# Reordering one step of a linear-attention stage: the next pair's maximum ahead of the last pair's sum, normed rows and keys ahead of the logits' copy, and a first load in two parts

## The chip, the cores and the metric

The kernel runs on one core of one Trainium2 chip. The metric is device time in microseconds (us) of one execution; lower is better. The core has a matrix engine (PE, with its weight loads shown apart as PEld), a vector engine (DVE), an activation engine (ACT), a general engine (POOL) and SP, which here only starts transfers. Each engine works through its own queue of instructions, and they wait for each other by semaphores.

## What is computed

The reference is a block of three residual layers over 4 x 2048 rows of 256 numbers: half of a mixture-of-experts layer, an attention layer, and half of the same mixture-of-experts layer again. The mixture layer sends every row to two of eight experts with a capacity; it is not touched here. The attention is of the linear kind: no row is compared with another row. Cut to what matters:

```python
q = _split_heads(x @ Wq + bq)            # 16 heads of 16 columns
v = _split_heads(x @ Wv + bv)
q = softmax(q, axis=-1) * s              # over the 16 columns of a head
k = softmax(q, axis=-2) * s              # over all rows of the batch
ctx  = einsum('bhnd,bhne->bhde', k, v)   # 16 x 16 per head and batch
attn = einsum('bhnd,bhde->bhne', q, ctx)
x = x + (attn @ Wo + bo)                 # x inside is the normed row
```

So `k` comes from `q`, and nothing of a batch can be given out before all 2048 of its rows have gone into `ctx`.

## The kernel before

The stages follow each other: the first router and the first expert stage (to about 921 us of the span), the attention (925 to 1171), the second routing, and the second expert stage. Only the attention is touched by the change.

There the 8192 rows lie as 64 tiles of 128 rows in `xw` (each 256 columns of the row and 16 of the second router's logits and weights). They are loaded from `acc`, the sum written by the first expert stage, in 16 transfers of four tiles each (L1124). The work goes in 32 pairs of tiles, eight pairs to a batch, by a loop over steps `i` that is a software pipeline: step `i` begins pair `i`, and holds later parts of the pairs before. The loop stands in a block of manual schedule for PE, DVE, ACT and POOL: what is emitted first comes first in the queue of its engine. The order of the calls in the loop is therefore the order of execution on each engine.

The parts, with their engines:

- `stats(2i+2, 2)`: mean and variance of the next pair's two tiles on DVE (L783, L784), then the inverse deviation on POOL (`ve` L157, `rstd` L158).
- `turn_x(i)`: four transposes of the rows on PE (`trx`, L791), copied by ACT (`xT`, L793).
- `project(i-1)`: eight matrix products on PE (`qp`, L799). `qp` has a single PSUM buffer of two banks; each bank holds 256 columns of q and 8 router logits of one tile.
- `logits_in(i-1)`: ACT copies the 8 logits a tile from `qp` into `xw` (L805).
- `largest(i-1)`: DVE scales and biases `qp` into `q` (two instructions, L810), takes the maximum of each head (`m`, L815), and POOL subtracts it (L816).
- `exp(i-2)`: ACT, in place (L819).
- `share(i-2)`: DVE sums the exponentials (`z`, L823) and inverts (`rz`, L825); POOL multiplies (L826). `q` is then the softmax.
- `keys(i-3)`: ACT takes the exponential of the softmax (`ek`, L832) and writes the two normed tiles into a ring of four (`xs`, L837).
- `turn_q(i-3)`: four transposes on PE (`trq`, L844), copied by ACT (`qT`, L846).
- `sums(i-3)`: eight products of keys and normed rows on PE, summed in `pc` over the eight pairs of a batch (L856).
- `context_1` to `context_4`: once per batch, from `pc` to the matrix `mo` (L867 to L906).
- `add_y(y)` and `take_y(y)` with `y = i - 12`: eight products on PE (`py`, L914, one buffer), added to `xw` by DVE (L924), with the statistics of the result (L926) and, every second pair, the norms on POOL.
- `choose_on`: the second router's choice, two of its small DVE steps at a time, and the norm of finished rows on ACT (L185).

So steps 3 to 11 carry everything but `add_y` and `take_y`; steps 12 to 31 carry all; the rest runs out.

Of the kernel before, what the change touches and what calls it, by code (L numbers as in the profile page):

```python
# [26 lines left out]
def macaron_kernel(  # L27
# [22 lines left out]
    nc = tc.nc  # L50
    B, N, D = x_in.shape
    E, _, F = wg.shape
    NJ = N // P
    T = B * NJ
# [15 lines left out]
    def tiles_of(ap):  # L70
        return ap.rearrange("(t p) d -> p t d", p=P)

    x_rows, out_rows = x_in.rearrange("b n d -> (b n) d"), out.rearrange("b n d -> (b n) d")
    x_tiles, out_tiles, acc_tiles = tiles_of(x_rows), tiles_of(out_rows), tiles_of(acc)
    JL = NJ // 4
# [15 lines left out]
        out=before, in_=ones, compare_op=ALU.is_gt, fill=0.0, base=0, pattern=[[1, P]], channel_multiplier=-1  # L91
# [4 lines left out]
        out=heads, in_=ones, compare_op=ALU.is_ge, fill=0.0, base=0,  # L96
# [3 lines left out]
        out=heads, in_=heads, compare_op=ALU.is_ge, fill=0.0, base=15,  # L100
# [36 lines left out]
    rstd = const.tile([P, T], F32, name="rstd")  # L137
# [13 lines left out]
    def spread(ap, shape):  # L151
        return ap.to_broadcast(shape)

    def deviation(var, n, pool, dst, scale=1.0):

        ve = pool.tile([P, NJ], F32, tag="ve", name="ve", bufs=4)
        nc.gpsimd.tensor_scalar(ve[:, :n], var, scale, EPS, ALU.mult, ALU.add)  # L157
        nc.gpsimd.tensor_tensor(dst, ve[:, :n], spread(minus_half, [P, n]), ALU.pow)  # L158
# [105 lines left out]
    def write_rows(xw, to, ts):  # L264
        nc.sync.dma_start(out=tiles_of(to)[:, ts, :], in_=xw[:, ts, :])
# [500 lines left out]
    def attention(xw, w, to, weights, pool, ppool):  # L766
# [7 lines left out]
        ring = []  # L774
# [5 lines left out]
        def stats(t, n):  # L780
            for i in range(t, t + n):
                st = pool.tile([P, 6], F32, tag="st", name="st", bufs=4)
                nc.vector.bn_stats(st, xw[:, i, 0:D])  # L783
                nc.vector.bn_aggr(mv[:, i, :], st)  # L784
            deviation(mv[:, t : t + n, 1], n, pool, rstd[:, t : t + n])
# [18 lines left out]
        def logits_in(i):  # L804
            nc.scalar.copy(xw[:, 2 * i : 2 * i + 2, D:W1], qp[i][:, :, D:W1])  # L805

        def largest(i):
            q = pool.tile([P, 2, D], F32, tag="q", name="q", bufs=5)
            for k in range(2):
                nc.vector.scalar_tensor_tensor(  # L810
                    q[:, k, :], qp[i][:, k, 0:D], rstd[:, 2 * i + k : 2 * i + k + 1], bqs, ALU.mult, ALU.add
                )
            qs[i] = q.rearrange("p k (h d) -> p (k h) d", d=H)
            m = pool.tile([P, 2 * H], F32, tag="m", name="m", bufs=3)
            nc.vector.tensor_reduce(m, qs[i], AX.X, ALU.max)  # L815
            nc.gpsimd.tensor_tensor(qs[i], qs[i], spread(m.unsqueeze(2), [P, 2 * H, H]), ALU.subtract)  # L816

        def exp(i):
            nc.scalar.activation(qs[i], qs[i], AF.Exp)  # L819

        def share(i):
            z = pool.tile([P, 2 * H], F32, tag="z", name="z", bufs=3)
            nc.vector.tensor_reduce(z, qs[i], AX.X, ALU.add)  # L823
            rz = pool.tile([P, 2 * H], F32, tag="rz", name="rz", bufs=3)
            nc.vector.reciprocal(rz, z)  # L825
            nc.gpsimd.tensor_tensor(qs[i], qs[i], spread(rz.unsqueeze(2), [P, 2 * H, H]), ALU.mult)  # L826

        def keys(i):


            eks[i] = pool.tile([P, 2, D], F32, tag="ek", name="ek", bufs=3)
            nc.scalar.activation(  # L832
                eks[i].rearrange("p k (h d) -> p (k h) d", d=H), qs[i], AF.Exp, scale=QSCALE
            )
            for k in range(2):
                t = 2 * i + k
                nc.scalar.mul(ring[i % 4][:, k, 0:D], xw[:, t, 0:D], rstd[:, t : t + 1])  # L837

        def turn_q(i):
            ps = ppool.tile([P, DC, 2, P], F32, tag="tr", name="trq", bufs=2)  # L840
# [24 lines left out]
        def context_1(b):  # L865
            rc = pool.tile([P, DC], F32, tag="rc", name="rc", bufs=2)
            nc.vector.reciprocal(rc, pcs[b][:, :, D])  # L867
            g = pool.tile([P, DC, D], F32, tag="g", name="g", bufs=1)
            nc.scalar.mul(g[:, 0, :], pcs[b][:, 0, 0:D], rc[:, 0:1])
            nc.vector.tensor_scalar(g[:, 1, :], pcs[b][:, 1, 0:D], rc[:, 1:2], None, ALU.mult)  # L870
            parts[b] = g
# [27 lines left out]
        def context_4(b):  # L899
            cxT = parts.pop(b)  # L900
            tag = "qp" if b == B - 1 else "py"
            ps = ppool.tile([P, 2, 2 * D], F32, tag=tag, name="mops", bufs=1)
            for k in range(DC):
                nc.tensor.matmul(ps[:, k, 0:W1], cxT[:, k, :], wox[:, k, :], start=True, stop=True)
            mo[b] = pool.tile([P, DC, W1], F32, tag="mo", name="mo", bufs=2)
            nc.vector.tensor_tensor(mo[b], ps[:, :, 0:W1], spread(box.unsqueeze(1), [P, DC, W1]), ALU.add)  # L906
# [34 lines left out]
        def choose_on(n, m, which=0):  # L941

            while len(choosing) > which and n:
                ts, steps, tiles = choosing[which]
                while n:
                    n -= 1
                    if next(steps, 0) == 0:
                        steps = None
                        break
                if steps is None and ts.stop > T - NJ:  # L950
                    chosen.append(choosing.pop(which))
                    continue
                for t in tiles[: m if steps else None]:
                    norm_row(xw, t)
                del tiles[:m]
                if steps is None:
                    write_rows(xw, to, ts)
                    choosing.pop(which)

        def has(i, n=NP):  # L960
            return 0 <= i < n

        LAST = NP + PB + 4
        with tc.manual_schedule(engines=ENGINES):
            stats(0, 2)
            for i in range(LAST):
                y = i - PB - 4

                b3 = (i - 3) // PB - 1 if (i - 3) % PB == 0 else -1
                b4 = (i - 4) // PB - 1 if (i - 4) % PB == 0 else -1  # L970
                if has(b3, B):
                    context_1(b3)
                if b3 == B - 1:
                    choose_on(1, 0)
                if has(b4, B - 1):
                    context_4(b4)
                if has(i - 2):
                    exp(i - 2)
                if has(i):
                    turn_x(i)  # L980
                if has(i - 2):
                    share(i - 2)
                if has(i + 1):
                    stats(2 * i + 2, 2)
                if has(i - 1):
                    project(i - 1)
                    logits_in(i - 1)
                if has(i - 3):
                    keys(i - 3)
                if has(b3, B):  # L990
                    context_2(b3)
                if b3 == B - 1:
                    choose_on(1, 0)
                if has(i - 1):
                    largest(i - 1)
                if has(i - 3):
                    turn_q(i - 3)
                ps = add_y(y) if has(y) else None
                if b3 == B - 1:
                    choose_on(3, 0)  # L1000
                if has(b3, B):
                    context_3(b3)
                if b3 == B - 1:
                    choose_on(2, 0)
                    context_4(b3)
                if has(i - 3):
                    sums(i - 3)
                if i < LAST - PB - 2:
                    choose_on(2, 2)
                if has(y):  # L1010
                    take_y(y, ps)
                if i >= LAST - PB:

                    choose_on({LAST - 3: 0, LAST - 2: 5, LAST - 1: 3}.get(i, 4), 0)
            while choosing:
                for k in reversed(range(len(choosing))):
                    choose_on(1, 0, k)
            for ts, _, tiles in chosen:
                for t in tiles:
                    norm_row(xw, t)  # L1020
                write_rows(xw, to, ts)
# [58 lines left out]
    with tc.tile_pool(name="w1", bufs=2) as wpool:  # L1080
        weights = {}
        with tc.tile_pool(name="r1", bufs=1) as pool, tc.tile_pool(name="r1p", bufs=2, space=PSUM) as ppool:
            xw = pool.tile([P, T, W], F32, name="xw")
# [36 lines left out]
    xw = kept.tile([P, T, W], F32, name="xw")  # L1120
    w = kept.tile([P, E, T], F32, name="w")
    with tc.tile_pool(name="at", bufs=1) as pool, tc.tile_pool(name="atp", bufs=1, space=PSUM) as ppool:
        for t in range(0, T, JL):
            nc.sync.dma_start(out=xw[:, t : t + JL, 0:D], in_=acc_tiles[:, t : t + JL, :])  # L1124
        attention(xw, w, rows[1], att_weights, pool, ppool)


# [41 lines left out]
```

## Time and profile before

| what | value |
|---|---|
| runs shown, median of 3 | 2053.22 us (2050.62 to 2053.68) |
| the profiled execution's own time | 2051.27 us |
| its span | 2049.4 us |
| PE, DVE, ACT, POOL busy over the span | 1879.1, 1413.5, 656.8, 882.3 us |
| mean granted clock of PE | 0.954 |
| loads of `xw` from `acc`, first issue | 924.97 us |
| first transposes of the attention | 928.95 us |
| first context product (L890) | 990.38 us |
| last product of `add_y` ends about | 1160.4 us |
| routing's first transposes (L282) | 1171.17 us |

The page of a profile sums over all stages, so busy shares of the whole span tell little of the 246 us in question. Times in the timeline are counted from the span's start. A line of the timeline has start, duration, engine, line, operation, tile written and tiles read, shapes, and in square brackets how long the engine had been idle and who ended that. Ends of matrix products are modelled.

### The profile page before, as it was taken

The numbers are of one execution on the slowest core, as the hardware profiler recorded it, in microseconds if no ns is written. First come the engines' busy times: TensorE is split into PE (matmuls) and PEld (weight loads), VectorE is DVE, ScalarE is ACT, GpSimd is POOL, SyncE is SP. The second block draws the span as 40 slices with busy tenths as digits, with TensorE's granted clock in tenths as the row PEclk, the third lists the DMA queues.
The fourth block names the chain that finished last, engine by engine and source line by source line (L and its number), as shares of the span: only waits on it lengthen the run. The fifth ranks groups of instructions, "written<-read, shape, count | busy, mean of one in ns | idle before, by whom it ended". The sixth has DMA issues, their size and how long they took to land.

```text
span 2049.4 us, 24693 instructions
## 1 busy us (share of the span) xinstructions
PE 1879.1 (92%) x9162; PEld 1439.7 (70%) x9162; DVE 1413.5 (69%) x2499; ACT 656.8 (32%) x1357; POOL 882.3 (43%) x737
## 2 busy tenths in 40 slices
PE   6379999999999999997999627999999999999998
PEld 4247777777777777775888415777777777777776
DVE  7867676767676766545789886767676666767654
ACT  5322322232223222224556503222322222232221
POOL 5335353535353535334556303535353535353533
PEclk8579999999999999998999858999999999999999
DMA  9912222223131322115012531223132323131211
GB/s 348 299 28 38 78 38 78 51 65 77 39 79 38 80 40 39 17 16 167 21 42 86 182 134 28 69 47 79 37 79 40 81 37 84 34 84 34 41 15 13
DMA packets 99910, 147.61 MB, mean 72 GB/s; under 512 B 7496, under 2 KB 86352, under 8 KB 99664
## 3 DMA queue, kind: packets, MB, share of 16 engines
q1 hardware_dynamic: 69056, 102.77, 14.8%
q0 software_dynamic: 30720, 43.27, 13.0%
q8 instruction: 72, 1.18, 0.2%
q14 instruction: 46, 0.38, 0.1%
q10 hardware_dynamic: 16, 0.01, 0.0%
HBM read 98.84 MB, written 55.57 MB: 75 GB/s over the span
## 4 chain that ended last, share of the span: by engine, by line
PE 83%; DVE 6%; POOL 2%; issue 1%; ACT 1%; DMA 1%; POOLq 0%; DVEq 0%; ACTq 0%; SPq 0%
PE mm L529 41%; PE mm L675 27%; PE one L529 7%; PE tr L476 2%; PE pc L856 2%; PE qp L799 2%; PE ix L399 1%; PE py L914 1%; DVE above L298 1%; DVE q L810 1%; DVE st L926 0%; DVE xw L924 0%; DVE cand L305 0%; DVE m L815 0%; PE trx L791 0%
## 5 line engine op out<-in xcount | busy, mean ns | idle before, releaser
L675 PE MATMUL mm<-wdt,h 128*128 128x256 f32 x2560 | 579.0, 381 | 0.0
L675 PEld LDWEIGHTS mm<-wdt,h 128*128 128x128 f32 x2560 | 475.9, 190 | 63.9
L561 POOL TENSOR_TENSOR h<-ct 128x1280 f32<-128x1280 f32 x96 | 279.0, 2906 | 424.7 <-ACT ct L558 421.5
L529 PE MATMUL mm<-xs,ws 128*128 128x320 f32 x1536 | 459.1, 435 | 2.2 <-DVE xs L482 2.0
L482 DVE TENSOR_TENSOR ct<-ct,mm 128x640 f32<-128x640 f32 x384 | 313.0, 818 | 104.2 <-PE mm L529 95.5
L529 PEld LDWEIGHTS mm<-xs,ws 128*128 128x128 f32 x1536 | 292.0, 191 | 127.0 <-issue 5.5
L558 ACT ACTIVATE ct<-ct 128x320 f32<-128x320 f32 (+1 forms) x224 | 181.8, 813 | 284.5 <-DVE ct L482 284.5
L482 DVE TENSOR_TENSOR ct<-p,mm 128x640 f32<-128x640 f32 x128 | 105.0, 821 | 238.5 <-ACT p L546 200.4
L482 DVE TENSOR_TENSOR ct<-u,mm 128x640 f32<-128x640 f32 x256 | 210.1, 821 | 59.7 <-PE mm L529 55.8
L546 ACT COPY p<-one 128x320 f32<-128x320 f32 x256 | 108.5, 424 | 406.4 <-PE one L529 404.2
L685 POOL DMA_INDIRECT out_dram<-eo,ixs x80 | 133.1, 1664 | 220.7 <-ACT eo L684 213.7
L685 POOL DMA_INDIRECT acc<-eo,ixs x80 | 132.8, 1661 | 221.1 <-ACT eo L684 214.1
L451 POOL DMA_INDIRECT r<-rows,ixs x160 | 158.6, 991 | 145.3 <-DVE ws L482 97.2
L684 ACT ACTIVATE eo<-mm,r 128x256 f32<-128x256 f32 x160 | 75.7, 473 | 396.5 <-PE mm L675 396.5
L529 PE MATMUL mm<-xsT,ws 128*128 128x320 f32 x512 | 158.7, 432 | 0.0
L390 DVE TENSOR_TENSOR lo<-count,slot_lo 128x1024 f16<-128x1024 int16 x112 | 128.3, 1220 | 0.0
L529 PEld LDWEIGHTS mm<-xsT,ws 128*128 128x128 f32 x512 | 97.3, 190 | 40.5
L482 DVE TENSOR_TENSOR u<-p,mm 128x640 f32<-128x640 f32 x128 | 104.9, 820 | 15.6 <-PE mm L529 12.5
L529 PE MATMUL one<-xsT,wgt 128*128 128x320 f32 x256 | 91.3, 439 | 0.0
L529 PE MATMUL mm<-xsT,wgt 128*128 128x320 f32 x256 | 91.1, 438 | 0.1
L529 PE MATMUL mm<-xsT,wut 128*128 128x320 f32 x256 | 90.9, 437 | 0.0
L529 PE MATMUL one<-xsT,wut 128*128 128x320 f32 x256 | 90.5, 435 | 0.0
(207 smaller groups left out, 2314.9 us busy)
## 6 DMA issues: line engine op xcount, KB each, us to landing
wgt<-in_L_ffn_wg_dram SPq DMA_DIRECT2D x16, 1024.0 KB, 5.0
wut<-in_L_ffn_wu_dram SPq DMA_DIRECT2D x16, 1024.0 KB, 7.0
wdt<-in_L_ffn_wd_dram SPq DMA_DIRECT2D x16, 1024.0 KB, 5.5
rows<-xw SPq DMA_DIRECT2D x7, 2176.0 KB, 10.6
xw<-in_L_attn_x_dram SPq DMA_DIRECT2D x16, 512.0 KB, 8.9
xw<-acc SPq DMA_DIRECT2D x16, 512.0 KB, 8.8
out_dram<-xw SPq DMA_DIRECT2D x16, 512.0 KB, 2.9
r<-rows,ixs POOLq DMA_INDIRECT x160
```

Source lines behind the costliest of these rows:

```text
L390: nc.vector.tensor_tensor(lo, spread(count.unsqueeze(1), shape), spread(at.unsqueeze(2), shape), ALU.is_equal)
L451: nc.gpsimd.indirect_dma_start(out=r, out_offset=None, in_=src[:, :], in_offset=bass.IndirectOffsetOnAxis(ap=lists[e][:, i : i + 1], axis=0),)
L476: nc.tensor.transpose(ps[:, (i - i0) * P : (i - i0 + 1) * P], got[k][i][:, c * P : (c + 1) * P], ident)
L482: nc.vector.tensor_tensor(o, a, b, op)
L529: nc.tensor.matmul(ps, a, b, start=True, stop=True)
L546: nc.scalar.copy(p1[p][:, m, :], one[:, :BH])
L558: nc.scalar.activation(ct[:, qs, 0, :], ct[:, qs, 0, :], AF.Silu)
L561: engine.tensor_tensor(hq[:, qs, :], ct[:, qs, 0, :], ct[:, qs, 1, :], ALU.mult)
L675: nc.tensor.matmul(po[i], hs[p][:, j, i * P : (i + 1) * P], weights[e][2][:, j * NF + p, :], start=(p == 0 and j == 0), stop=(p == NF - 1 ...
L684: nc.scalar.mul(eo, po[i], got[k][i][:, D + e : D + e + 1])
L685: ins = nc.gpsimd.indirect_dma_start(out=dst[:, :], out_offset=bass.IndirectOffsetOnAxis(ap=lists[e][:, i0 + i : i0 + i + 1], axis=0), in_ ...
L799: nc.tensor.matmul(qp[i][:, k, 0:W1], xT[i][:, k, c, :], wqx[:, c, :], start=(c == 0), stop=(c == DC - 1))
```

## The change

Three edits, all in the attention stage.

1. `share(i-2)` moves from before `stats` to behind `largest(i-1)`. On DVE the order of a step turns from z, rz, statistics, q, q, m to statistics, q, q, m, z, rz. On POOL the multiplication by `rz` moves from the head of the step to behind the subtraction of the maximum.
2. `keys(i-3)` moves from behind `logits_in(i-1)` to before `project(i-1)`, and inside it the two normed tiles are written before the exponential. On ACT the order of a step turns from exp, xT, logits' copy, ek, xs, xs, qT to exp, xT, xs, xs, ek, logits' copy, qT.
3. The first load of four tiles becomes two loads of two tiles each; there are 17 transfers instead of 16.

No instruction of an engine is added or taken away, PE's order stays, and nothing is computed otherwise.

```diff
         def keys(i):
+            for k in range(2):
+                t = 2 * i + k
+                nc.scalar.mul(ring[i % 4][:, k, 0:D], xw[:, t, 0:D], rstd[:, t : t + 1])
             eks[i] = pool.tile([P, 2, D], F32, tag="ek", name="ek", bufs=3)
             nc.scalar.activation(
                 eks[i].rearrange("p k (h d) -> p (k h) d", d=H), qs[i], AF.Exp, scale=QSCALE
             )
-            for k in range(2):
-                t = 2 * i + k
-                nc.scalar.mul(ring[i % 4][:, k, 0:D], xw[:, t, 0:D], rstd[:, t : t + 1])
...
                 if has(i):
                     turn_x(i)
-                if has(i - 2):
-                    share(i - 2)
                 if has(i + 1):
                     stats(2 * i + 2, 2)
+                if has(i - 3):
+                    keys(i - 3)
                 if has(i - 1):
                     project(i - 1)
                     logits_in(i - 1)
-                if has(i - 3):
-                    keys(i - 3)
...
                 if has(i - 1):
                     largest(i - 1)
+                if has(i - 2):
+
+                    share(i - 2)
                 if has(i - 3):
                     turn_q(i - 3)
...
-        for t in range(0, T, JL):
-            nc.sync.dma_start(out=xw[:, t : t + JL, 0:D], in_=acc_tiles[:, t : t + JL, :])
+
+        for t, n in [(0, 2), (2, 2)] + [(t, JL) for t in range(JL, T, JL)]:
+            nc.sync.dma_start(out=xw[:, t : t + n, 0:D], in_=acc_tiles[:, t : t + n, :])
```

## The prediction

> **What bounds the kernel now.** I read the views from the whole to the step. The page first: TensorE is busy 92% of the span and the chain that ended last is 83% PE, nearly all of it in the two expert stages that the change leaves alone. The attention stage runs from 924.97 us (first load) to about 1171, so whatever is won must come from 246 of 2049 us. Next, the busy times in stretches of 20 us (columns: stretch, length, then PE, PEld, DVE, ACT, POOL busy with counts, granted clock, DMA share, GB/s):
>
> ```profile
> 960.00:980.00 20.00, 17.01 (x88) 13.99 (x87) 13.32 (x36) 11.80 (x28) 10.57 (x15) 1.00 0.00 1
> ...
> 1020.00:1040.00 20.00, 20.00 (x107) 17.28 (x106) 16.66 (x44) 10.17 (x24) 12.08 (x22) 1.00 0.10 33
> ```
>
> There are two halves. From 1000 to about 1123 PE never rests (one step each 6.17 us: qp starts at 1000.62 and 1006.79). Only before, in the steps without add_y, and in the run-out does it have holes. The waits of PE name them:
>
> ```profile
> PE pc L856 <- ACT xs L837: 5.9, 8, 0.8
> ...
> PE qp L799 <- DVE q L810: 3.7, 2, 3.0
> ```
>
> Then the timeline of one early step, between two exponentials:
>
> ```profile
> 954.09 0.63 ACT L819 ACTIVATE q<-q 128x512 f32<-128x512 f32 x1 [1.63 <-POOL q L816]
> 954.62 0.57 ACT L793 COPY xT<-trx 128x512 f32<-128x512 f32 x1
> 954.75 0.69 DVE L823 TENSOR_REDUCE z<-q 128x32 f32<-128x512 f32 x1 [1.83 <-ACT q L819]
> ...
> 955.90 0.17 ACT L805 COPY xw<-qp 128x16 f32<-128x16 f32 x1 [0.71 <-PE qp L799]
> ...
> 955.97 0.63 ACT L832 ACTIVATE ek<-q 128x512 f32<-128x512 f32 x1
> ...
> 956.50 0.90 ACT L837 ACTIVATE xs<-xw,rstd 128x256 f32<-128x256 f32 x2
> ...
> 956.77 0.86 DVE L810 SCALAR_TENSOR_TENSOR q<-qp,rstd,bqs 128x256 f32<-128x256 f32 x2
> ...
> 957.05 2.00 PE L856 MATMUL pc<-xs,ek 128*128 128x257 f32 x8 [0.75 <-ACT xs L837]
> ...
> 957.66 0.69 DVE L815 TENSOR_REDUCE m<-q 128x32 f32<-128x512 f32 x1
> ...
> 958.43 1.06 POOL L816 TENSOR_TENSOR q<-q,m 128x512 f32<-128x512 f32 x1 [0.35 <-DVE m L815]
> ```
>
> Two loops of nearly one length turn here. On DVE: exp, z, rz, statistics (1.03), q, q, m, the subtraction on POOL, exp again: 954.09 to 959.52, 5.43 us. On PE: qp (1.95, its end to the copy .03), copy of the logits (its successor .07 later), ek (.53), first xs (.50 and .05), pc to trx 1.84, trx to qp .44: 5.41 us. PE alone needs 1.84 + .44 + 1.78 + .44 = 4.50 us by the same starts.
>
> One more look decides the forecast: what q waits for when DVE is free.
>
> ```profile
> 1014.95 0.17 ACT L805 COPY xw<-qp 128x16 f32<-128x16 f32 x1 [1.14 <-PE qp L799]
> ...
> 1015.22 0.88 DVE L810 SCALAR_TENSOR_TENSOR q<-qp,rstd,bqs 128x256 f32<-128x256 f32 x2 [0.23 <-POOL q L826]
> ```
>
> DVE had been idle since 1014.99 and qp ended at 1014.91, yet q starts .27 after the start of ACT's copy, .10 after its end. The same .27 stands at 935.02, 1002.87, 1009.04, 1021.39 and 1033.74, and no q starts before the copy of its step has ended. A DVE read of a PE result otherwise starts .04 after PE's end (py ends 1004.78, its sum starts 1004.82). The releaser named (POOL) had nothing for q: q waits for the logits' copy.
>
> **What the Trainium skill says.** "PSUM — Partial Sum Buffer", section "PSUM bank collisions raise a hardware error": two engines may not touch one bank together, a ScalarE read with a VectorE read included, so accesses must be held apart by semaphores. That fits: columns 0 to 255 (q) and 256 to 263 (copy) share qp's banks, and the trace shows the .27. "TensorE: Matmul & The Clock Gate", section "Architectural detail": ACT and DVE are strict FIFO; every row above agrees, so emission order is execution order. The same page, Part 1: after an idle window of about 3.4 us PE's clock halves. Here PE idles from 938.5 to 941.48 and the granted clock is 0.50 from 942 to 945; qp there takes 3.57 against 1.95. "DMA: Bandwidth & Descriptors", section "Anatomy of one DMA", gives about 2.0 us fixed for one transfer; here first issue to first use is 3.9 us, of which 0.52 MB at 350 GB/s is 1.5, leaving 2.4.
>
> **The change, part by part.**
>
> *Largest ahead of share.* Nothing is added. On DVE z and rz (.69 and .35) go behind q, q, m; on POOL the multiplication by rz goes behind the subtraction. q no longer waits for z, hence not for the exponential of the step before: the 5.43 loop on DVE is cut. What is later: q's final value by about 1.1 us after the subtraction (rz ends 2.65 after q's start, the product runs from 2.83 to 3.90). trq needs it in the next step, some 4 us after q at the earliest; ek needs it at 4.58 (below). Both are covered.
>
> *Keys ahead of the logits' copy.* On ACT the order becomes exp, xT, xs, xs, ek, copy, qT. pc no longer waits for qp's end by way of ACT, so the 5.41 loop is cut too. But the copy now stands behind exp, and q behind the copy. That closes a new loop, one step long: q to m .89, m .69, to the subtraction .08 to .14, the subtraction 1.06, to exp .03 (in all 2.77 at 935.02 to 937.79, 2.82 at 984.54 to 987.36); exp to xT .53, xT to the next .47, xs .40 and .40, ek .53 (2.33); copy to q .27. Sum 5.37 to 5.42. So both old loops are replaced by one just as long, and PE keeps about .7 us of hole in each early step. The steady pace gains only what DVE had slipped: q went from 945.90 to 984.54 in seven steps, 5.52 each; 7 x (5.52 - 5.39) = .9 us.
>
> *First rows in two transfers.* The first pair's data is half, .26 MB at 350 GB/s: .75 us earlier; bounds 0 (if both halves land together) and 1.0. One more issue costs SP .37 us while its queue is only these loads; the next tiles are needed a step later.
>
> *The start.* With the first rows .75 earlier, q of pair 0 starts at 934.27 and its exp at 937.04. Then xT 937.57, copy of pair 1 938.03 (qp of pair 1, behind q as before, ends about 937.32), q of pair 1 938.30 against 940.47 before, since z, rz and the statistics no longer stand ahead. Its exp 941.07, copy of pair 2 943.40, q 943.67 against 945.90: 2.23 us ahead, the .75 included. qp of pair 2 can start at 939.2, so the long idle and its half clock go too, but ACT's chain, not PE, ends last there; I count nothing for the clock.
>
> *Later steps.* 2.23 + .9 = 3.1 us ahead when the first context product starts (990.38 before). From there PE is the bound at 6.17, and the new loop of 5.4 fits under it with .75 to spare. In the steps with choosing, DVE is busy up to 93%; its order is only rotated, so the sum of y comes at the same place when DVE is behind. Twice the choosing's own exponential on ACT waits for DVE steps that now stand 1.04 later, which I bound at .5 us of PE each; I take 0, since PE's work ahead of pc (trq and py, 2.2 us) covers it. The other way, the waits of z for exp (.18 to .50 at six late steps) vanish, which helps only where DVE ends last; I take .3. In the run-out (1125 to 1134), where DVE is the bound, q must now wait for a copy, about .4 us lost. Sum: 3.1 - .4 + .3 = 3.0 us gained. What follows the attention shifts as a whole.
>
> Against the profiled execution (2051.27, span 2049.4) that is 2048.3. The median shown is 2053.22, 1.95 above it, so I say 2050.0.
>
> **Rivals.**
>
> *A, the bound moves as above*: -3.0, with 1.5 to 4.8 by the unknowns (transfer 0 to 1.0, clock phase ±1, choosing -1).
>
> *B, q isn't tied to the copy.* Then the loop is two steps long: q to exp 2.80, exp to pc 2.48, pc to the end of the next qp 4.23, 9.51 for two, 4.76 a step. pc of pair 0 would start at 942.6 instead of 946.23 and seven steps win .65 each: 8.2 us, 2045. For it: PE's named waits are exactly those removed. Against it: the six cases of .27.
>
> *C, the start wins more.* PE's clock turned full at about 935.0; if the earlier rows let it turn one window (3.4 us) sooner, qp of pair 0 ends up to 1.6 us earlier: 4.6 in all, 2048.6.
>
> *S, slower.* The new loop ties DVE, POOL and ACT in one ring through the late half as well, where ACT also has two norm rows (.98) and POOL the norms' row of five small operations (1.9 us every second step). If these fall inside the ring by more than .75 us, it exceeds 6.17 and decides: at 1.4 us over 13 choosing steps it costs 13 x .65 = 8.5, net +5.5, 2058.7. For it: POOL starts the subtraction .76 late at 1117.67 for this reason. Against: norm rows stand ahead of exp, where ACT mostly waits .9 to 2.9 us anyway.
>
> *N, nothing*: transfer and start are given back in the choosing steps, 2053.
>
> **How the numbers follow.** A .60, B .12, C .10, S .15, N .03. No-change is within 0.2%, 4.1 us. Of A a quarter lies beyond that (.15): faster .15 + .12 + .10 = .37; slower .12 of S; same .51. The range leaves out S's .12 and about half of B: 2044 to 2056.
>
> **What would show it.** Right: early steps still 5.4 us apart; before each early pc PE waits for ACT ek instead of xs; q .27 after the copy, and the copy right behind ek; q of pair 1 at about 938.3, the first context product near 987.2; the late steps 6.17. Wrong: early steps of 4.8 (B), holes of PE in front of pc or py after 1000 (S), full clock before 933 (C), first trx no earlier than 928.9 (no gain from the split).

## The result, and the profile after

The changed kernel took 2056.11 us (median of 22 runs) against 2052.70 for the kernel before (22 runs beside it): ratio 1.0018, 95% interval 1.0009 to 1.0026. The profiled spans are 2054.4 and 2049.4 us. The change made the kernel slower by 0.18%; the forecast, 2050.0 against a median of 2053.22, was 0.16% faster.

To see where, the attention is cut at marks that both traces have: the first issue of a load, the starts of `q` on DVE (L810) of single pairs (numbered 0 to 31), and the first transposes of the second routing (L282, 1171.17 us before and 1175.52 after).

| stretch | before, us | after, us | difference |
|---|---|---|---|
| first load to q of pair 0 | 10.05 | 7.55 | -2.50 |
| q of pair 0 to q of pair 10 | 55.02 | 52.74 | -2.28 |
| pair 10 to pair 17 | 43.70 | 43.87 | +.17 |
| pair 17 to pair 31, the steps with the choice | 92.30 | 98.90 | +6.60 |
| pair 31 to the routing | 45.13 | 46.11 | +.98 |
| sum | 246.20 | 249.17 | +2.97 |

So the start won more than was forecast, and one stretch gave it all back and more. Another 1.4 us of the span lie ahead of the first load (924.97 and 926.35), where no line was changed. Each stretch is read from one profiled execution. From pair 17 to pair 31 four kernels with the same order there agree within .02 us (before, e3, e6 and e7 below); the start scatters, which is treated further down.

First the profile after, in stretches of 20 us (columns as before: length, busy time of PE, PEld, DVE, ACT and POOL with counts, granted clock, DMA share, GB/s):

```profile
960.00:980.00 20.00, 17.72 (x94) 14.47 (x92) 13.25 (x35) 10.46 (x25) 11.34 (x16) 1.00 0.00 1
1060.00:1080.00 20.00, 18.17 (x90) 14.57 (x89) 19.45 (x50) 10.57 (x25) 11.87 (x21) 1.00 0.09 30
```

The first line is slightly fuller on PE than before (17.72 against 17.01). The second is the damage: PE works 18.17 of 20 us and DVE 19.45, where the same stretch of before had 20.00 and 18.55:

```profile
1060.00:1080.00 20.00, 20.00 (x106) 17.32 (x105) 18.55 (x57) 12.37 (x29) 12.66 (x22) 1.00 0.16 53
```

The waits of PE in the attention (us in total, times, longest) agree:

```profile
PE pc L856 <- ACT xw L805: 5.9, 8, 0.8
PE trq L844 <- POOL q L826: 4.6, 5, 1.7
...
PE py L914 <- DVE xw L924: 2.3, 5, 1.5
```

The first is the wait for the keys under another name: the same 5.9 us in 8 times that stood at `xs` (the copy of the logits is the ACT row that ends beside `ek`; in the step below `ek` ends at 953.85 and `pc` starts at 953.90). Of the other two, the first is new and the second was 2.1 us in 2 times before: PE waits for the softmax's product on POOL and, more often, for the sum of y on DVE.

An early step of the changed kernel, in its timeline (start, duration, engine, line, tiles, and in brackets the idle time ahead and who ended it):

```profile
951.42 0.63 ACT L819 ACTIVATE q<-q 128x512 f32<-128x512 f32 x1 [2.38 <-POOL q L816]
...
952.42 0.91 ACT L833 ACTIVATE xs<-xw,rstd 128x256 f32<-128x256 f32 x2
...
953.23 0.62 ACT L835 ACTIVATE ek<-q 128x512 f32<-128x512 f32 x1
953.75 0.16 ACT L805 COPY xw<-qp 128x16 f32<-128x16 f32 x1
...
954.01 0.88 DVE L810 SCALAR_TENSOR_TENSOR q<-qp,rstd,bqs 128x256 f32<-128x256 f32 x2 [1.76 <-ACT xw L805]
...
956.78 0.63 ACT L819 ACTIVATE q<-q 128x512 f32<-128x512 f32 x1 [2.38 <-POOL q L816]
```

This is the ring of the forecast: exponential to exponential 5.36 us, `q` .26 behind the start of a copy for which DVE stood idle 1.76 us.

### The profile page after: what moved, and what is told of

Its sections match the earlier page's. It is cut to its first block, busy times and chain, and to the rows that moved or that the text cites. A ratio compares the mean times of both kernels' runs of the same rounds, so it can differ in the third digit from the quotient of the medians.

```text
span 2054.4 us, 24695 instructions
## 1 busy us (share of the span) xinstructions
PE 1881.0 (92%) x9162; PEld 1437.0 (70%) x9162; DVE 1417.5 (69%) x2499; ACT 656.1 (32%) x1357; POOL 883.0 (43%) x737
## 4 chain that ended last, share of the span: by engine, by line
PE 81%; DVE 6%; issue 4%; ACT 2%; POOL 1%; DMA 1%; POOLq 0%; SPq 0%; DVEq 0%; ACTq 0%
PE mm L529 40%; PE mm L675 27%; PE one L529 7%; PE tr L476 2%; PE ix L399 1%; PE py L914 1%; PE pc L856 1%; DVE q L810 1%; DVE m L815 1%; PE qp L799 1%; DVE st L926 1%; DVE xw L924 1%; ACT xs L833 1%; POOL q L816 0%; DVE z L823 0%
```

## The experiments

Two theories for the 6.60 us, and they don't exclude each other:

- RING: the one-step ring (`q`, maximum, subtraction, exponential, `xT`, `xs`, `ek`, copy, `q`) is broken into by ACT's other work in the late steps, so that DVE stands idle at `q` for the copy.
- PORT: `z`, `rz` now run ahead of the choice on DVE, so POOL's multiplication by `rz` follows its subtraction at once. Both then stand beside the choice's small DVE operations, and these get longer.

That the order alone is slow, choice or not, is the rival of both. The Trainium skill, "SBUF — State Buffer", section "Who interferes with whom", speaks for PORT: a DVE instruction with two SBUF inputs contends with a GpSimd (POOL) instruction that reads SBUF, and the page calls the ports that the two share an exclusive lock. In the lines below such a DVE operation ends just behind POOL's. From pair 20 to pair 25 the trace of before shows at most one such operation a step, the trace after two. Before, around one subtraction on POOL:

```profile
1069.93 0.28 DVE L215 TENSOR_TENSOR tmp<-tmp,rev 128x128 f32<-128x128 f32 x1
1070.13 0.17 DVE L215 TENSOR_TENSOR b<-b,rs 128x16 f32<-128x16 f32 x1
1070.15 1.06 POOL L816 TENSOR_TENSOR q<-q,m 128x512 f32<-128x512 f32 x1 [0.41 <-DVE m L815]
...
1070.45 0.80 DVE L218 SCALAR_TENSOR_TENSOR sm<-rs,b 128x16 f32<-128x16 f32 x1
```

After, the same part of the choice:

```profile
1068.62 1.06 POOL L816 TENSOR_TENSOR q<-q,m 128x512 f32<-128x512 f32 x1 [0.58 <-DVE m L815]
...
1069.38 0.45 DVE L215 TENSOR_TENSOR tmp<-tmp,rev 128x128 f32<-128x128 f32 x1
1069.64 1.11 POOL L826 TENSOR_TENSOR q<-q,rz 128x512 f32<-128x512 f32 x1
...
1069.75 1.03 DVE L215 TENSOR_TENSOR b<-b,rs 128x16 f32<-128x16 f32 x1
...
1070.90 0.16 DVE L218 SCALAR_TENSOR_TENSOR sm<-rs,b 128x16 f32<-128x16 f32 x1
```

A product of 128x16 numbers takes .17 us before and 1.03 after; it ends at 1070.78, POOL's multiplication at 1070.75. `sm` goes the other way, .80 to .16: before, it was the one beside the subtraction (ends 1071.25 and 1071.21).

All kernels below were measured against the kernel before on the same chip; medians of different sets don't compare, ratios do. By the ratios the changed kernel and e1 are slower than before, e5, e6, e7 and e9 faster; e2, e3, e4 and e10 can't be told from it. Their stretches, cut as above (us; "context" is pairs 17 to 20 and 25 to 28, where a batch's context is worked out, "choice" pairs 20 to 25 and 28 to 31):

| kernel | ratio (95%) | load to pair 0 | 0 to 10 | 10 to 17 | context | choice | 31 to routing |
|---|---|---|---|---|---|---|---|
| before | 1 | 10.05 | 55.02 | 43.70 | 41.67 | 50.63 | 45.13 |
| after | 1.0018 (1.0009-1.0026) | 7.55 | 52.74 | 43.87 | 44.51 | 54.39 | 46.11 |
| e1 | 1.0009 (1.0001-1.0018) | 9.32 | 51.36 | 45.11 | 41.50 | 54.27 | 46.11 |
| e2 | 1.0006 (.9997-1.0014) | 9.21 | 55.02 | 43.78 | 41.58 | 51.68 | 45.26 |
| e3 | 1.0001 (.9992-1.0009) | 8.66 | 55.02 | 43.70 | 41.67 | 50.62 | 46.61 |
| e4 | .9998 (.9989-1.0006) | 8.17 | 52.76 | 43.87 | 43.77 | 51.69 | 45.74 |
| e5 | .9981 (.9973-.9988) | 8.04 | 46.40 | 44.49 | 41.24 | 54.18 | 47.56 |
| e6 | .9985 (.9979-.9992) | 8.13 | 52.76 | 43.79 | 41.67 | 50.63 | 45.28 |
| e7 | .9948 (.9935-.9962) | 7.93 | 46.41 | 44.69 | 41.66 | 50.64 | 45.28 |
| e8 | one run | 8.65 | 52.73 | 43.86 | 41.49 | 48.88 | 53.66 |
| e9 | .9972 (.9965-.9979) | 7.95 | 46.41 | 44.48 | 42.66 | 49.89 | 47.43 |
| e10 | 1.0005 (.9996-1.0013) | 9.50 | 55.26 | 44.99 | 41.11 | 50.77 | 46.20 |

### One edit at a time: e1, e2, e3

e1 is the kernel before with the share behind the largest alone:

```diff
-                if has(i - 2):
-                    share(i - 2)
                 if has(i + 1):
                     stats(2 * i + 2, 2)
...
                     largest(i - 1)
+                if has(i - 2):
+                    share(i - 2)
```

> Only the first edit (share behind largest); ACT's order and the load as before. Theory PORT: in the steps with choosing, POOL's subtraction and multiplication now run back to back and each holds up the choice's small two-input operations on DVE; so the choosing steps slow down here as in the changed kernel, to about 7.0 us against 6.17, and the kernel is 4 to 8 us slower than before less a start gain of about 1 us: +3 to +6. Rival RING (q waits for the logits' copy, which waits for the keys): that ring isn't closed here, the choosing steps stay at 6.17, and the kernel is within 2 us of before. Early steps: 5.41 in both theories, since pc still waits by way of copy and ek.

e2 is the kernel before with the keys alone moved (both parts of that edit), e3 with the first load alone in two:

```diff
+                if has(i - 3):
+                    keys(i - 3)
                 if has(i - 1):
                     project(i - 1)
                     logits_in(i - 1)
-                if has(i - 3):
-                    keys(i - 3)
```

> Only the second edit (normed rows and keys ahead of the logits' copy); DVE's and POOL's order and the load as before. Theory PORT: choosing steps stay at 6.17 and the time within 2 us of before; early steps stay near 5.43, since z still stands ahead of q on DVE. Rival RING: the choosing steps go above 6.5 and the time 3 us or more above before.

> Only the third edit (first load in two parts). All theories: first transposes 2.7 us after the first load's issue instead of 3.9, everything else as before; 1.2 us faster at most, too little to tell in the time of the whole.

Measured: 2050.24 (e1), 2048.16 (e2) and 2046.49 us (e3) against 2047.85. The share alone costs 3.64 us in the choice (54.27) and nothing in the context; with 3.66 won from pair 0 to 10, 1.41 of it given back at the first context (pairs 10 to 17), it still ends slower. The forecast of 3 to 6 us for the whole was too high (1.8 by the ratio), because the early gain was put at 1 us. The keys alone win nothing early (55.02, as before) and cost 1.05 in the choice. The load alone wins 1.39 us to pair 0 and keeps it through pair 31, but loses 1.48 after it: PE's clock in 1125 to 1150 is .93 against 1.00. Neither single edit shows the 2.84 us that the whole change costs in the context: for that both moves are needed.

### The two theories crossed: e4, e5, e9

e4 is the changed kernel with the share behind the choice's two steps, so that POOL's multiplication is out of their way; RING stays:

```diff
                     largest(i - 1)
-                if has(i - 2):
-
-                    share(i - 2)
...
                     choose_on(2, 2)
+                if has(i - 2):
+                    share(i - 2)
```

> The changed kernel with share put behind the step's choosing (choose_on), still ahead of take_y: z, rz and POOL's multiplication come after the choice. Theory PORT: the choice then stands beside the subtraction alone, as before the change, and the choosing steps fall from 7.0 to about 6.2 to 6.5; the early gain stays, so 2 to 4 us faster than before. Rival ROTATION (the sum of y is late because z and rz stand ahead of it, whatever POOL does): z and rz still stand ahead of it, the choosing steps stay at 7.0 and the time 3 us above before. Rival RING: also 7.0.

e5 is the changed kernel with the logits' copy behind `q`, so that no `q` waits for a copy; PORT stays:

```diff
                     project(i - 1)
-                    logits_in(i - 1)
...
                     largest(i - 1)
+                    logits_in(i - 1)
```

> The changed kernel with the logits' copy emitted behind largest, so that q on DVE no longer waits for ACT's copy (the copy now waits for q). If q's wait for the copy is what set the pace of the early steps (5.36 to 5.42 us in the changed kernel), they fall to about 4.8, PE alone needing 4.5, and the first context product comes some 4 us earlier, 56 to 57 us after the first load's issue against 60.8. Late part, theory PORT AND RING (both cost): the ring's share goes and PORT's stays, so about 4 to 5 us above before as in the kernel with the first edit alone, against 7.7 in the changed kernel. Rival RING ALONE: the late part falls to that of before. In all about 3 to 5 us faster than the changed kernel, 0 to 4 faster than before.

e9 has both edits.

> The changed kernel with both remedies in all steps: share behind the choosing, and the logits' copy behind largest. If the 7.7 us lost in the late part are two costs (the choice beside POOL's pair, and q behind the copy), both are gone: the late part from the first context product to the last batch's first sum falls from 162.9 us (159.1 with either remedy alone) to 155 to 156, as before the change. If either remedy only shifts one common cost (z and rz ahead of the sum of y), it stays at 158 to 159.

Measured: 2046.49 us (e4, against 2047.85), 2044.09 (e5, against 2047.32), 2041.50 (e9, against 2046.62). From pair 17 to 31, with 92.30 before:

| | multiplication beside the choice | multiplication behind it |
|---|---|---|
| `q` behind the copy | after: 98.90, +6.60 | e4: 95.46, +3.16 |
| copy behind `q` | e5: 95.42, +3.12 | e9: 92.55, +.25 |

Taking away either cause takes away half, taking away both leaves .25 (.99 more than before in the context, .74 less in the choice). The two causes nearly add up, and they lie in different steps: e5 removes 3.27 us in the context (44.51 to 41.24) and .21 in the choice, e4 removes 2.70 in the choice and .74 in the context. For the whole, e4 was forecast 2 to 4 us faster than before and isn't, since the ring's part stays; e5's 0 to 4 us came true (3.9 by the ratio).

What PORT does to DVE is seen in the five steps of the first batch's choice, pair 20 to pair 25. Of before and after two views each, all engines and then line L215 alone (DVE): before,

```profile
1055.28:1088.16 32.88, 32.88 (x170) 28.40 (x170) 30.91 (x91) 22.81 (x52) 20.79 (x36) 1.00 0.17 55
...
1055.28:1088.16 32.88, 3.57 (x9) 1.00 0.17 55
```

after,

```profile
1052.82:1088.02 35.20, 33.15 (x165) 27.15 (x164) 33.99 (x91) 22.23 (x50) 19.94 (x32) 1.00 0.13 43
...
1052.82:1088.02 35.20, 6.40 (x9) 1.00 0.13 43
```

and e4, line L215 alone:

```profile
1050.92:1083.66 32.74, 3.56 (x9) 1.00 0.14 46
```

The same 91 DVE instructions take 30.91 us before and 33.99 after (the steps 6.58 and 7.04 us on average); 2.83 of the 3.08 more are the nine two-input operations of L215. With the multiplication behind the choice they are back at 3.56. The steps grew by less (2.32) because DVE had 1.97 us of idle time there.

What RING does is seen in the step of pair 20 after:

```profile
1048.38 0.71 DVE L215 TENSOR_TENSOR ex<-ex,mx 128x128 f32<-128x128 f32 x1
...
1049.12 0.31 ACT L230 ACTIVATE ex<-ex 128x128 f32<-128x128 f32 x1 [3.37 <-DVE ex L215]
1049.34 1.07 ACT L185 ACTIVATE xw<-xw,shift,rstd 128x256 f32<-128x256 f32 x2
...
1050.32 0.61 ACT L819 ACTIVATE q<-q 128x512 f32<-128x512 f32 x1
...
1052.64 0.15 ACT L805 COPY xw<-qp 128x16 f32<-128x16 f32 x1
...
1052.82 0.88 DVE L810 SCALAR_TENSOR_TENSOR q<-qp,rstd,bqs 128x256 f32<-128x256 f32 x2 [1.26 <-ACT xw L805]
```

ACT stands 3.37 us at the choice's own exponential (1.41 before), which needs DVE's `ex`; the norm's rows follow, then exp, and behind it in ACT's queue the keys and the copy. DVE has caught up meanwhile and idles 1.26 us at `q`, on its way into the steps of the choice, where it has little to spare (busy 30.91 of 32.88 us before). In before the copy of this step came at 1054.21 and `q` at 1055.28, as soon as DVE was free. At pairs 18 and 26 the same is done by the context's `g` (ACT, L869), which waits for PE's sums by way of DVE and stands ahead of exp: DVE idles .89 us at `q` each time. Where the loss lies is seen against e5. Of its 3.27 us, 2.7 are in the two steps with the choice's exponential (into pairs 20 and 28, 7.75 us each after and 6.40 in e5) and .57 in pairs 25 to 27; the idle time at pair 18 cost nothing, pairs 17 to 19 take 14.57 us after and 14.56 in e5.

### The order without the choice: e8

The changed kernel with `choose_on(2, 2)` taken out of the loop; the choice is made in the run-out instead, nothing is left out.

```diff
-                if i < LAST - PB - 2:
-                    choose_on(2, 2)
```

> The changed kernel without the second router's choice inside the main steps (all of it is made in the run-out instead, so the run-out is far longer and the whole slower by 10 us or more; only the late steps count). Theory PORT: without the choice's two-input operations there is nothing on DVE for POOL's pair of operations to hold up, and the late steps 20 to 31 fall from about 7.0 to 6.17, context steps apart. Rival RING ALONE: the ring through copy, q, subtraction, exp, keys is still closed and POOL still has its norms, so the late steps stay above 6.5.

One run: 2049.58 us. The choice stretch falls to 48.88, below before's 50.63 though the order of the other work is that of the change; `q` follows `q` at 6.17 to 6.18 us from 1041.78 to 1078.83. The rest comes back in the run-out (53.66 against 46.11), though the whole is 2.3 us above before's 2047.32 and not the 10 forecast. So the order by itself isn't slow; it is slow beside the choice.

### One more POOL operation, alone: e10

The kernel before, with one more 128x512 product on POOL behind the subtraction in the late steps. It works on a tile of zeros that nobody reads.

```diff
                     largest(i - 1)
+                    if i >= PB + 4:
+                        nc.gpsimd.tensor_tensor(idle, idle, spread(bqs.unsqueeze(1), [P, 2, D]), ALU.mult)
```

> The kernel before, orders untouched, with one more POOL operation of the subtraction's size (128x512, on a tile of zeros that nothing reads) right behind the subtraction in steps 12 to 32. Theory PORT: the choice on DVE then stands beside two POOL operations in a row as in the changed kernel; its two-input operations take up to 1 us instead of .3, and the choosing steps go from 6.17 to about 6.5 to 7, 3 to 6 us in the late part (155.2 before). Rival: POOL doesn't hold DVE up; POOL itself has room (about 3.8 us busy of 6.17 a step, 4.9 with the addition), so the late part stays within 1 us of 155.2.

Measured: 2048.30 us against 2046.62, and pair 17 to 31 took 91.88, no longer than before. The 3 to 6 us forecast there are missed, and the trace tells why (lines of the attention have numbers 2 higher in e10):

```profile
1070.76 1.06 POOL L818 TENSOR_TENSOR q<-q,m 128x512 f32<-128x512 f32 x1 [0.41 <-DVE m L817]
...
1071.05 0.80 DVE L218 SCALAR_TENSOR_TENSOR sm<-rs,b 128x16 f32<-128x16 f32 x1
1071.78 0.69 DVE L926 TENSOR_TENSOR xw<-xw,py 128x528 f32<-128x528 f32 x1
1071.78 1.27 POOL L999 TENSOR_TENSOR idle<-idle,bqs 128x512 f32<-128x512 f32 x1
```

The choice's operation was held by the subtraction, as before, and DVE was through with the choice when the new product began. It ran beside the sum of y, which reads one input from PSUM and took its usual .69. But in four places of this run the new product did meet a DVE operation with two SBUF inputs, and held it. Two of them, a difference of the norms' statistics and, in the run-out, a product of the choice:

```profile
1031.45 1.28 POOL L999 TENSOR_TENSOR idle<-idle,bqs 128x512 f32<-128x512 f32 x1
...
1031.72 1.03 DVE L170 TENSOR_TENSOR ndif<-st 128x4 f32<-128x4 f32 x1
...
1130.23 1.31 POOL L999 TENSOR_TENSOR idle<-idle,bqs 128x512 f32<-128x512 f32 x1
...
1130.34 1.23 DVE L215 TENSOR_TENSOR rs<-rs,sm 128x16 f32<-128x16 f32 x1
```

Both take .17 us when POOL is at nothing, and both end within .05 us of a product whose result nobody reads. So no result of POOL is waited for; an unrelated POOL operation is enough. (Three of the four places lie in pairs 10 to 17, ahead of any choice, which took 1.29 us longer than before.) In the attention of the twelve traces 155 such DVE operations (of the choice, and the sums and differences of L170 to L173) began while POOL was at a product or subtraction of 128x512: 147 were lengthened and ended .02 to .24 us behind POOL's, the other eight began in its last .14 us. More POOL work isn't the price in itself, then; it has to stand beside two-input DVE work.

### The change where it pays: e6, e7

e6 uses the new order in the steps ahead of the first sum of y only, and the old one after; e7 also puts the logits' copy behind `q` in those early steps. Both load in two.

```diff
+                early = i < PB + 4
+                if has(i - 2) and not early:
+                    share(i - 2)
...
+                if has(i - 3) and early:
+                    keys(i - 3)
                 if has(i - 1):
                     project(i - 1)
+                if has(i - 1) and not early:
                     logits_in(i - 1)
+                if has(i - 3) and not early:
+                    keys(i - 3)
...
                     largest(i - 1)
+                    if early:
+                        logits_in(i - 1)
+                if has(i - 2) and early:
                     share(i - 2)
```

(e6 is without the two lines that make the copy wait for `early`.)

> The new order only in the steps without add_y (i < 12), the old order of share and keys from step 12 on; the load in two parts. All theories: start as in the changed kernel (first context product about 60.8 us after the first load's issue, 4.7 earlier than before), late part as before: about 4.5 us faster than before, ratio 0.998.

> The kernel with the new order only in early steps, and there also the logits' copy behind largest. If the copy ahead of q paces the early steps: early steps about 4.8, first context product 56 to 57 us after the issue, late part as before: 8 to 9 us faster than before, ratio 0.996. If something else paces them: as the kernel with the new order in early steps only, 4.5 us faster.

Measured: 2045.59 us (e6) and 2037.33 (e7) against 2047.32. Both have before's late stretch to the hundredth or two (92.30), and keep the start. e6 wins 3.1 us by the ratio where 4.5 were forecast, e7 somewhat more than its 8 to 9. e7 is 10 us faster than before, 0.52% (0.38 to 0.65), and beats both kernels of this case. Its early steps are those of e5, here two `q` in a row:

```profile
960.44 0.88 DVE L810 SCALAR_TENSOR_TENSOR q<-qp,rstd,bqs 128x256 f32<-128x256 f32 x2 [0.89 <-PE qp L799]
...
961.41 0.17 ACT L805 COPY xw<-qp 128x16 f32<-128x16 f32 x1 [0.20 <-DVE q L810]
...
965.58 0.88 DVE L810 SCALAR_TENSOR_TENSOR q<-qp,rstd,bqs 128x256 f32<-128x256 f32 x2 [1.54 <-PE qp L799]
```

`q` waits for `qp` now, the copy for `q`, and the steps alternate between 4.5 and 5.1 us.

## Why the prediction was wrong, point by point

| term of the sum | forecast, us | measured |
|---|---|---|
| first rows in two transfers | -.75 | -1.26 (first issue to first transposes 3.98, then 2.72) |
| PE's clock at the start (rival C) | 0 | -1.28 (`qp` of pair 0 took 3.89, then 2.61) |
| pair 0 to pair 2 | -1.48 | -1.49 |
| pair 2 to pair 9 | -.9 | -.88 |
| pair 9 to pair 17 | 0 | +.26 |
| the late steps | -.3 | +6.60 |
| the run-out | +.4 | +.98 |

**Start and early steps.** The mechanism and the pace were right: two old loops replaced by one ring of 5.36 to 5.42 us (forecast 5.37 to 5.42), PE still waiting 5.9 us ahead of `pc`. The load was worth more than its share of bytes. Over all twelve kernels the first load is 7.55 to 8.66 us ahead of q of pair 0 where it was split and 9.21 to 10.05 where not, 1.4 us by the means. The clock was full from about 932, before the 933 named as rival C's sign, but it is a matter of phase: `qp` of pair 0 took 3.67 us in e3, which splits the load, and 3.10 in e1, which doesn't. The Trainium skill, "TensorE: Matmul & The Clock Gate", Part 1, says that the clock follows activity in a free-running window of about 3.4 us; when within its first products a stage meets the window's end is then not set by the stage, and the scatter from 2.61 to 3.89 us agrees, as does the granted clock, which turns full 3.0 to 6.1 us after the first transposes in the twelve traces. Rival C's mechanism is seen, but it can't be credited to the edit; in this trace it was luck. (In before the half clock came back after 2.98 us without a matrix product, 938.5 to 941.48, less than one such window.)

**The tie of q to the copy.** Right, and the basis of rejecting rival B. e5 turns it round: with the copy behind `q`, pair 0 to 10 takes 46.40 instead of 52.74, .63 us less a step, and pairs 3 to 9 are 4.81 us apart, where B's working had 4.76. What B took for given, e7 brings about.

**The late steps: the step that failed.** "In the steps with choosing, DVE is busy up to 93%; its order is only rotated, so the sum of y comes at the same place when DVE is behind." The rotation keeps every DVE instruction, but not its duration: PORT makes the same 91 instructions 3.08 us longer, and the choice stretches +3.76 in all. The trace of before had the warning, an addition of 128x16 numbers that took .80 us where a product of the same size took .17. I read the engine's busy share as a fixed sum of durations. Nor was 6.17, to which the forecasts compare the steps with the choice, their pace before: from pair 20 to 25 that was 6.58, and 7.04 after.

**The ring's spare time.** "The new loop of 5.4 fits under it with .75 to spare" holds for pairs 12 to 17 (6.17 us a step, as forecast) and without the choice (e8). It fails where ACT stands at something else of its queue ahead of exp. The choice's own exponential was bounded at .5 us each time and put at 0, because PE's work ahead of `pc` would cover it. The two steps took 7.75 us each where before took 6.83, so .92 each: what wasn't asked for is DVE, which stands idle at `q` behind the late copy (1.26 us). The context stretches, +2.84, are this (1.84) and pairs 25 to 27 (1.15), less .14 at pairs 17 to 19.

**Rival S** named the right side and a ring that exceeds the step, and it priced a net of +5.5 us against +2.97 measured in the attention. It had RING on 13 choosing steps by way of norm rows and POOL's small operations; RING acts in single steps around each batch's context, where ACT waits for the choice or the context, and the other half of the loss was no ring at all. So S was half right, and PORT was in none of the rivals.

**The run-out.** +.98 against .4, and not for the reason given, a wait of `q` for the copy: in the changed kernel DVE is idle for .01 us at most ahead of the last three `q`. e2, which has the copy behind the keys but the share in its old place, has +.13, and e1, whose copy stays ahead of the keys, has the same 46.11 as the change. So it belongs to the share's place. e3, e5 and e9 lose 1.5 to 2.4 us there, and these three alone have a stretch of 3.4 us at half clock between 1136 and 1145, seen as .93 in 1125 to 1150; e4 has 1.00 there and loses .6. What brings the half clock on in these three stays open.

## What to carry to other kernels

When instructions are only moved, ask of each what runs beside it on POOL at its new place: a small DVE operation with two SBUF inputs can be held until the POOL operation that it meets has ended. A copy that hands a shared PSUM bank to another engine ties two queues together; put it behind the reader on the critical engine, and that engine no longer waits for it. A reordering that wins in one phase of a software pipeline needn't be used in the next; a condition on the step kept most of the early gain here (8.6 us to pair 10, of which 1.0 was given back by pair 17) and lost nothing from there to pair 31.

## What the runs showed of the hardware that was not expected

- A DVE product of 128x16 took 1.03 us instead of .17, one of 128x128 .98 instead of .25, beside POOL operations of 1.11 us on 128x512 that share no data with them. A sum with one input from PSUM (.69) and the reduction to `z` (.68) took no longer beside such operations.
- Not every POOL operation that reads SBUF holds: in the trace of before the .25 product (L215, 1077.04) runs wholly beside POOL's power of 128x2 (L158, 1076.75 to 1077.54) and isn't lengthened, and so it went in all 58 meetings with L158 alone (128x2 or 128x4) in the attention of the twelve traces. By the rule cited above it would contend too; no wait is seen. What decides between the two, size or something else, wasn't tried.
- Splitting the first 0.52 MB load brought the first transposes 1.26 us nearer to the first issue, more than the .75 us that half the bytes take at 350 GB/s (351 were moved from 928 to 945 in before). Over the twelve kernels they come 2.72 to 2.91 us after it where the load was split and 3.98 to 4.04 where not.
